# Four layers on one core: a feed-forward residual summed on GpSimd, displaced temporaries, and fewer GpSimd blocks in two selective scans

## The chip, the core and the metric

The kernel runs on one core of a Trainium2 chip. The metric is the device time of one execution in microseconds. A core has TensorE (PE in the profile, with its weight loads as PEld), VectorE (DVE), ScalarE (ACT), GpSimd (POOL) and SyncE (SP), which here only issues DMAs. All engines run their own instruction lists in order and wait for each other on semaphores. A TensorE result lands in PSUM; VectorE and ScalarE read PSUM, and GpSimd works on SBUF alone.

## The reference, cut to what matters

The input is an image batch of shape (4, 64, 128, 128) in float32, and four layers follow each other. Layer 0 is a state-space ("mamba") block with 16 states. Layer 1 is a windowed spectral mixing. Layer 2 is two 3x3 convolutions with a channel gate. Layer 3 is two convolutions, a mamba block with 64 states, and a feed-forward block. The change touches layer 0, the mamba block of layer 3 and the feed-forward block of layer 3.

```python
def step(h, inp):                       # over the 16384 positions of an image
    d_t, b_t, c_t, u_t = inp
    dA = jnp.exp(d_t[..., None] * A)                       # A: (128, states)
    h = h * dA + (d_t * u_t)[..., None] * b_t[:, None, :]
    y = jnp.einsum('bdn,bn->bd', h, c_t)
    return (h, y)
...
y = selective_scan(silu(conv(xin)), softplus(dt), A, Bm, Cm, D) * silu(z)
...
t = t + mamba(layernorm(t), ...)                           # layer 3
t = t + pvt2ffn(layernorm(t), ...)   # fc1, depthwise 3x3, gelu, fc2
return x + y                         # y: t as an image; x: the input of layer 3
```

The last line is the residual of the change: the feed-forward result has both `t` (kept in DRAM as `s3`) and the layer's input (`x3`) added to it.

## The kernel before

**The scans.** Class `_Mamba` serves layer 0 and layer 3. A chunk is 1024 positions; there are 64 chunks. The 128 inner channels are split into 4 quarters `j`, and the states are taken 4 at a time as a group `g`. One iteration is one pair (group, quarter), 128 partitions (4 states by 32 channels) by 1024 positions. A chunk of layer 0 has 4 groups and 16 iterations ("narrow"), a chunk of layer 3 has 16 groups and 64 iterations ("wide"). Each iteration needs these steps:

- ScalarE makes `da = exp(dl * A)` (L595), up to 7 buffers ahead.
- TensorE puts the input term `bx` into one of 3 PSUM tiles. In a group of kind "D" it spreads B over the partitions (L533) and VectorE multiplies by `du` (L539). In a group of kind "A" the products `bxT` were made beforehand in transposed form, and TensorE transposes them (L527).
- VectorE runs the recurrence as one scan over 1024 positions into one of 8 slots of `ring` (L640).
- GpSimd multiplies the scan's result by C, in the tile `cb` (L646), and after four iterations copies the last column to `state` (L648).
- TensorE sums over the states into `y` (L470), three iterations after the group ended.

**Who makes `bxT`.** A group's `bxT` has 8 blocks of 128 positions. For a whole block one GpSimd instruction serves all 4 states (L444); a block on ScalarE takes 4 instructions (L440). The list `mine` says how many of the 8 blocks GpSimd takes, by the distance of the group from the last "D" group. In layer 0 the kinds are D A D A and `mine` is (2,). In layer 3 they are D A A A four times and `mine` is (4, 2, 2), so 32 blocks a chunk. `run` paces the ScalarE part by a credit, so that it is done 4 iterations before its group.

**The pieces of the next chunk.** The convolution, the gates, the step size, B and C of the next chunk (`front`, `middle`), and the projection and norms of the last one (`behind`), are cut into pieces. The dictionary `slots` gives the iteration, relative to the chunk's first, at whose end a piece's TensorE part is issued; its ScalarE read follows one iteration later ("next"). A piece borrows one of the PSUM tiles from the `bx` pool (`take`, `give`). Where `slots` has "conv2", the convolution is issued in two halves. From the read of the convolution until the read of "v", `hold` keeps back the exponentials of L595. The order that `run` writes is pinned on each engine.

**Temporaries.** `tmp` hands out [128, 1024] tiles with one tag; some users split such a tile into two halves of 512 columns. `cb` is a tile of 1025 columns used from column 1. Tiles start on multiples of 32 bytes, so `cb` stands 4 bytes off `ring` modulo 32, while other operand pairs (`pos` and `xc` of L347, the halves of `nx` in L1527 and of `no` in L1566) stand a multiple of 32 bytes apart.

**The feed-forward block** (`layer3_ffn`). It works on 32 strips of 16 image rows. `first` computes fc1 of the strip after into `h1` and `h0`: GpSimd clears the edge columns (L1657, L1658), ScalarE writes the inside (L1671). `taps` does half of the depthwise convolution as 9 VectorE instructions (L1688, L1686); the other half runs on TensorE (L1735). `second` does fc2 and adds bias and residual on VectorE (L1701), then stores (L1704). The residual tile `res` is loaded by four DMAs from `s3` on SP; four DMAs issued by GpSimd add `x3` to it (both L1726), each after its load has landed. In SP's order a strip's stores (L1704) are followed by the load of `N` (L1645) and the loads of the next `res`. In GpSimd's order the four accumulating DMAs come before the memsets of the next `h1` and `h0`.

Of the kernel before, what the change touches and what calls it, by code (L numbers as in the profile page):

```python
# [10 lines left out]
F32 = mybir.dt.float32  # L11
AF = mybir.ActivationFunctionType
ALU = mybir.AluOpType
# [4 lines left out]
P = 128  # L18
B, C, HH, WW = 4, 64, 128, 128
HW = HH * WW  # L20
TC = 1024
# [149 lines left out]
class _Mamba:  # L171
# [131 lines left out]
        return self.wp.tile([P, w], F32, name=name, tag=name, bufs=bufs)  # L303

    def tmp(self, name):
        return self.wp.tile([P, TC], F32, name=name, tag="tmp", bufs=self.bufs["tmp"])


    def front(self, c, S, read, before_silu=None):
# [108 lines left out]
        self.read.add(id(t))  # L418

    def _C(self, c, g):  # L420
        t = self.t("cb", 3, TC + 1)[:, 1:]
        for q in range(NQ):
            n = NQ * g + q
            self.nc.sync.dma_start(t[DD * q : DD * (q + 1)], c["C"][n : n + 1, :].to_broadcast([DD, TC]))
        return t
# [266 lines left out]
@with_exitstack  # L692
def layer0(ctx, tc, K, w, x, x1):
    nc = tc.nc
    slots = {"conv": -24, "z": -22, "v": -20, "C": -16, "B": -14, "duT": -12, "project": 32, "rstd": 34}
    m = _Mamba(ctx, tc, K, 16, w, "DADA", {"xc": 2, "sz": 3, "tmp": 4, "bc": 2, "soon": (), "da": 7, "made": 0, "mine": (2,)}, slots)
    cp, wp = m.cp, m.wp
    eps = cp.tile([P, 1], F32, name="eps")
    nc.vector.memset(eps, 1e-5)
# [79 lines left out]
        finish.append(last)  # L779

    chunks = [{"at": divmod(i * TC, HW), "reset": i == 0} for i in range(B * HW // TC)]
    m.run(chunks, ahead, behind, 24)
    flush()


# [693 lines left out]
def layer3_mamba(ctx, tc, K, w, t3, s3, n3):  # L1479

    nc = tc.nc
    slots = {"centre": -47, "norm": -45, "conv": -32, "conv2": -31, "z": -30, "v": -29, "C": -16, "B": -14, "duT": -12, "project": 80, "centre2": 82, "norm2": 84}
    m = _Mamba(ctx, tc, K, 64, w, "DAAADAAADAAADAAA", {"xc": 1, "sz": 2, "tmp": 4, "bc": 1, "soon": (), "da": 7, "made": 7, "mine": (4, 2, 2)}, slots)
    cp = m.cp
    eps = cp.tile([P, 1], F32, name="eps3")
    nc.vector.memset(eps, 1e-5)
# [17 lines left out]
    def ahead(c):  # L1504
        if c is chunks[0]:
            load(c)
        t0 = c["at"][1]
        S = m.t("S", 1, TC + 3)
        no = m.tmp("nx")
        xs, sq = no[:, :512], no[:, 512:]  # L1510
        yield m.slot(c, "centre")
        pm = m.take(0)
        m.mm(pm, (K.cent, c["X"]))
        if c is not chunks[-1]:
            load(chunks[c["no"] + 1])
        yield "next", 0
        nc.scalar.activation(xs, pm, AF.Copy, scale=g1)
        nc.scalar.activation(sq, pm, AF.Square)
        m.give(pm)
        yield m.slot(c, "norm")  # L1520
        pm = m.take(0)
        m.mm(pm, (K.j2, sq))
        yield "next", 0
        _rstd(nc, sq, pm, eps)
        m.give(pm)
        yield "next", 0
        nc.gpsimd.tensor_mul(xs, xs, sq)  # L1527
        nc.gpsimd.tensor_copy(S[:, :3], tail if t0 else pad.to_broadcast([P, 3]))
        for h in range(2):
            nc.gpsimd.tensor_copy(tail[64 * h : 64 * (h + 1), : 3 - h], xs[64:, 509 + h :])  # L1530
        yield "next", 0
        yield "next", 0
        for k in range(2):
            for h in range(NH):
                at = 3 - k + 512 * h
                nc.sync.dma_start(S[64 * k : 64 * (k + 1), at : at + 512], xs[64 * h : 64 * (h + 1)])
        yield from m.front(c, S, lambda: None)

    def behind(c, yg):
        b, t0 = c["at"]  # L1540
        tr = m.tmp("tx")[:, :512]
        for h in range(NH):
            nc.sync.dma_start(tr[64 * h : 64 * (h + 1)], _halves(t3[b], t0)[h])
        yield m.slot(c, "project")
        pm = m.take(1)
        m.project(pm, woT, yg, tr)
        yield "next", 0
        nc.scalar.copy(tr, pm)
        m.give(pm)
        yield m.slot(c, "centre2")  # L1550
        pm = m.take(1)
        m.mm(pm, (K.cent, tr))
        yield "next", 0
        no = m.tmp("no")
        xs, o = no[:, :512], no[:, 512:]
        nc.scalar.copy(xs, pm)
        nc.scalar.activation(o, pm, AF.Square)
        m.give(pm)
        yield m.slot(c, "norm2")
        pm = m.take(1)  # L1560
        m.mm(pm, (K.j2, o))
        yield "next", 0
        _rstd(nc, o, pm, eps)
        m.give(pm)
        yield "next", 0
        nc.gpsimd.tensor_mul(o, xs, o)  # L1566
        for h in range(NH):
            nc.sync.dma_start(_halves(s3[b], t0)[h], tr[64 * h : 64 * (h + 1)])
            nc.sync.dma_start(_halves(n3[b], t0)[h], o[64 * h : 64 * (h + 1)])

    chunks = [{"at": (b, t0), "reset": t0 == 0} for b in range(B) for t0 in range(0, HW, TC)]
# [4 lines left out]
def layer3_ffn(ctx, tc, K, w, n3, s3, x3, out):  # L1576
# [4 lines left out]
    nc = tc.nc  # L1581
# [134 lines left out]
    for n, (b, r0) in enumerate(strips):  # L1716
# [4 lines left out]
        ahead = first(n + 1, H)  # L1721
        res = wp.tile([P, 2, 4, WW], F32, name="res3", tag="res3", bufs=3)
        ximg = x3[b].rearrange("c (r w) -> c r w", w=WW)
        for eng, img, add in ((nc.sync, simg, ALU.bypass), (nc.gpsimd, ximg, ALU.add)):
            for q in range(R // 4):
                eng.dma_start(res[half[q % 2], q // 2], img[:, r0 + 4 * q : r0 + 4 * q + 4, :], accum_op=add)  # L1726
        g0 = [wp.tile([P, 4, WW], F32, name=f"g0{q}", tag=f"g0{q}") for q in range(NR)]
        o = wp.tile([P, 2, 4, WW], F32, name="o3", tag="o3")
        pd = [dp.tile([P, 4, WW], F32, name=f"pd{q}", tag=f"pd{q}") for q in range(NR)]
# [127 lines left out]
```

## Time and profile before

| what | us |
|---|---|
| median of 3 runs (lowest, highest) | 17136.39 (17125.25, 17164.81) |
| the profiled execution, its own time | 17161.19 |
| its span, first to last instruction | 17159.4 |
| layer 0's scan, window 77 to 3185 | 3108 |
| layer 3's scan, window 5153 to 16065 | 10912 |
| feed-forward block, window 16160 to 17159 | 999 |

The profiled execution lies 24.80 us above the median, and 1.79 us of its time lie outside its span. Busy time is read stage by stage, since the stages have different limits. An instruction's duration can overlap the next one's by some tens of ns, so sums of durations come out a little above busy time. The page calls ScalarE's and VectorE's waits by the last releaser that it can see.

### The profile page before, as it was taken

The page shows a single profiled execution, that of the slowest core. Times are in us where ns is not written, and L with a number is a line of the kernel's source. Part 1 is how long each engine was busy: PE and PEld are TensorE (multiplying, and loading weights), DVE is VectorE, ACT ScalarE, POOL GpSimd, SP SyncE. Part 2 cuts the span into 40 slices and gives each one's busy share as a digit, 9 for nine tenths or more (in the row PEclk, how much of TensorE's full clock was granted, in tenths as well). Part 3 has the DMA queues.
Part 4 walks back from the last instruction along what each step waited for, and adds up shares of the span by engine and source line. Part 5 has one row for each costly group of instructions (what it writes and reads, how often), then busy time and mean ns, then how long its engine had stood idle before and what let it go on. Part 6 is the DMA issues. An engine that isn't in the chain of part 4 may idle for free.

```text
span 17159.4 us, 249842 instructions
## 1 busy us (share of the span) xinstructions
PE 13728.5 (80%) x85562; PEld 7134.6 (42%) x85562; DVE 15207.3 (89%) x8587; ACT 13644.9 (80%) x27884; POOL 13844.1 (81%) x9954
## 2 busy tenths in 40 slices
PE   7888888899987777777777777777777777777766
PEld 3333333388434444444444444444444444444312
DVE  7999999732879999999999999999999999999766
ACT  7888888411539999999999999999999999999532
POOL 6888888501449999999999999999999999999511
PEclk8888888889999999999889999999999999999888
DMA  6666666311343333333333333333333333333233
GB/s 161 175 174 175 173 176 176 105 43 44 119 141 91 97 85 96 87 96 86 96 86 96 88 96 86 98 89 93 89 94 90 93 90 94 91 92 89 66 67 66
DMA packets 705600, 1779.59 MB, mean 104 GB/s; under 512 B 202481, under 2 KB 246465, under 8 KB 694849
## 3 DMA queue, kind: packets, MB, share of 16 engines
q1 hardware_dynamic: 694080, 1746.83, 37.4%
q0 software_dynamic: 10240, 16.79, 0.7%
q8 instruction: 672, 11.01, 0.3%
q14 instruction: 608, 4.97, 0.1%
HBM read 1439.91 MB, written 289.41 MB: 101 GB/s over the span
## 4 chain that ended last, share of the span: by engine, by line
PE 32%; DVE 26%; ACT 15%; issue 10%; DMA 7%; POOL 4%; SPq 4%; DVEq 0%; POOLq 0%; ACTq 0%
DVE ring L640 18%; ACT bxT L440 7%; PE y L470 7%; PE bx L527 6%; PE bx L300 5%; ACT da L595 5%; DVE bx L539 4%; DVE g L1686 3%; PE bx L533 3%; PE m L1247 3%; POOL ring L646 2%; DMA du<-d 2%; SPq L566 2%; DMA d<-pos 1%; DMA dl<-d 1%
## 5 line engine op out<-in xcount | busy, mean ns | idle before, releaser
L640 DVE TENSOR_TENSOR_SCAN ring<-da,state,bx 128x1024 f32<-128x1024 f32 x4848 | 11037.2, 2329 | 206.2 <-PE bx L527 110.3
L646 POOL TENSOR_TENSOR ring<-ring,cb 128x1024 f32<-128x1024 f32 x5120 | 10219.1, 2016 | 550.6 <-DVE ring L640 311.8
L440 ACT ACTIVATE bxT<-duT,BT 128x128 f32<-128x128 f32 x19456 | 6038.3, 389 | 23.7 <-PE bx L527 22.9
L595 ACT ACTIVATE da<-dl,A 128x1024 f32<-128x1024 f32 x5120 | 5732.2, 1139 | 362.6 <-DVE ring L640 347.0
L527 PE MATMUL bx<-cst,bxT 128*128 128x128 f32 x28672 | 4316.8, 298 | 1138.1 <-DVE ring L640 1047.7
L527 PEld LDWEIGHTS bx<-cst,bxT 128*128 128x128 f32 x28672 | 3771.9, 210 | 2616.7 <-DVE ring L640 1605.2
L470 PE MATMUL y<-ring,cst 128*32 128x512 f32 x20480 | 2971.1, 661 | 103.0 <-POOL ring L646 103.0
L444 POOL TENSOR_TENSOR bxT<-duT,BT 128x512 f32<-128x512 f32 x2304 | 2391.5, 1049 | 9.9 <-ACT BT L384 9.9
L533 PE MATMUL bx<-bc,spread 64*128 64x512 f32 (+1 forms) x6144 | 1810.0, 686 | 627.0 <-DVE ring L640 624.3
L539 DVE TENSOR_TENSOR bx<-du,bx 128x1024 f32<-128x1024 f32 x1536 | 1852.4, 1213 | 458.5 <-PE bx L533 315.6
L470 PEld LDWEIGHTS y<-ring,cst 128*32 128x32 f32 x20480 | 630.1, 117 | 1841.9 <-issue 1251.3
L533 PEld LDWEIGHTS bx<-bc,spread 64*128 64x128 f32 (+1 forms) x6144 | 523.3, 198 | 1730.3 <-DVE ring L640 1204.8
L300 PE MATMUL bx<-S,cw 128*128 128x512 f32 x1024 | 668.0, 813 | 376.4 <-DVE ring L640 363.2
L1726 POOL DMA_DIRECT2D res<-d_x x128 | 106.4, 1256 | 923.1 <-DMA res<-d_s 922.1
L1247 PE MATMUL m<-V,cw 64*64 64x512 f32 x6144 | 715.7, 604 | 87.9 <-POOL V L1233 49.0
L1137 POOL TENSOR_TENSOR xs<-xs,cl 128x1024 f32<-128x1024 f32 x32 | 75.9, 2372 | 795.8 <-DVE cl L1136 795.8
L1671 ACT ACTIVATE h<-ph,ff_fc_b 128x384 f32<-128x384 f32 (+1 forms) x384 | 200.4, 574 | 598.4 <-PE ph L1666 575.5
L640 DVE TENSOR_TENSOR_SCAN ring<-da,bx 128x1024 f32<-128x1024 f32 x272 | 602.6, 2267 | 20.4 <-PE bx L527 11.2
L1686 DVE SCALAR_TENSOR_TENSOR g<-h,dww,g 128x2048 f32<-128x2048 f32 x256 | 602.0, 2352 | 11.3
L300 PEld LDWEIGHTS bx<-S,cw 128*128 128x128 f32 x1024 | 257.3, 264 | 783.0 <-DVE ring L640 466.7
L1735 PE MATMUL pd<-h,diag 32*32 32x512 f32 x9216 | 376.9, 671 | 191.8 <-POOL h L1658 162.7
L1247 PEld LDWEIGHTS m<-V,cw 64*64 64x64 f32 x6144 | 331.4, 136 | 470.2 <-issue 342.9
(341 smaller groups left out, 10271.5 us busy)
## 6 DMA issues: line engine op xcount, KB each, us to landing
cb<-c SPq DMA_DIRECT2D x5120, 128.0 KB, 2.9
dl<-d SPq DMA_DIRECT2D x2048, 128.0 KB, 3.0
du<-d SPq DMA_DIRECT2D x2048, 128.0 KB, 3.8
d<-pos SPq DMA_DIRECT2D x128, 512.0 KB, 4.2
d<-u SPq DMA_DIRECT2D x128, 512.0 KB, 3.9
S<-nx SPq DMA_DIRECT2D x256, 128.0 KB, 2.4
S<-in_x SPq DMA_DIRECT2D x120, 256.5 KB, 4.1
res<-in_x SPq DMA_DIRECT2D x128, 128.0 KB, 2.9
```

Of the source, the lines that this page charges most:

```text
L300: self.nc.tensor.matmul(out[: l.shape[1], k : k + 512], l, r[:, k : k + 512], start=i == 0, stop=i == len(pairs) - 1)
L440: nc.scalar.activation(t[:, k, q].rearrange("p e j -> p (e j)"), c["duT"][:, k, :], AF.Copy, scale=c["BT"][:, k, n : n + 1])
L444: nc.gpsimd.tensor_mul(t[:, k].rearrange("p q e j -> p q (e j)"), c["duT"][:, k].unsqueeze(1).to_broadcast(shape), c["BT"][:, k, NQ * g : ...
L470: nc.tensor.matmul(c["y"][DD * j : DD * (j + 1), _COLS[h]], K.sel, hc[:, _COLS[h]], start=False, stop=u["g"] == self.ng - 1,)
L527: nc.tensor.transpose(bx[:, P * m : P * (m + 1)], v["bxT"][:, m, :, :, j].rearrange("p q e -> p (q e)"), self.K.eye)
L533: nc.tensor.matmul(bx[:, _COLS[h]], self.spread[v["g"]][r], self.rows(v["c"]["B"], h, 0), start=True, stop=True)
L539: nc.vector.tensor_mul(tiles[k], v["c"]["du"][j], tiles[k])
L595: nc.scalar.activation(das[nexp], v["c"]["dl"][k], AF.Exp, scale=self.A[:, k, v["g"] : v["g"] + 1])
L640: nc.vector.tensor_tensor_scan(hs, das.pop(i), tiles[i], 0.0 if u["c"].get("reset") else st, ALU.mult, ALU.add)
L646: nc.gpsimd.tensor_mul(hc, hs, u["cb"])
L1247: self.nc.tensor.matmul(p[k][i][half[h]], U[half[i], k, x, :], V[half[i], k, NP * h : NP * (h + 1), x : x + WW], start=x == 0, stop=x == 2,)
L1686: nc.vector.scalar_tensor_tensor(g1, tap, wk, g1, ALU.mult, ALU.add)
```

## The change

Five edits are made together.

1. In the feed-forward block `x3` is loaded by four more plain DMAs on SP into a new tile `xin` (used from column 2), and one GpSimd addition over [128, 1024] puts it into `res`. GpSimd issues no DMA there any more.
2. `tmp` tiles of layer 3 become 1025 columns wide and are used from column 1 (`shift` 1; 0 in layer 0). The tiles that were split into two halves are now split at column 513 (`split`), so that the halves stand 4 bytes off each other.
3. `cb` is used from column 2 of 1026.
4. `mine` becomes (1,) in layer 0 and (4, 1, 2) in layer 3: one GpSimd block a group in the narrow chunk, 28 blocks in the wide one. In the whole program L444 goes from 2304 to 1920 instructions and L440 from 19456 to 20992.
5. The slots: layer 0 gets "conv" at -25 and a "conv2" at -24 (it was whole, at -24), "v" goes from -20 to -21 and the lead from 24 to 26. In layer 3 "conv" and "conv2" go one iteration earlier, to -33 and -32, "project" from 80 to 76 and "centre2" from 82 to 80.

```diff
     def tmp(self, name):
-        return self.wp.tile([P, TC], F32, name=name, tag="tmp", bufs=self.bufs["tmp"])
+        k = self.bufs["shift"]
+        return self.wp.tile([P, TC + k], F32, name=name, tag="tmp", bufs=self.bufs["tmp"])[:, k:]
+
+    def split(self, name):
+
+        t = self.wp.tile([P, TC + 1], F32, name=name, tag="tmp", bufs=self.bufs["tmp"])
+        return t[:, :512], t[:, 513:]
...
     def _C(self, c, g):
-        t = self.t("cb", 3, TC + 1)[:, 1:]
+        t = self.t("cb", 3, TC + 2)[:, 2:]
...
 def layer0(ctx, tc, K, w, x, x1):
-    slots = {"conv": -24, "z": -22, "v": -20, "C": -16, "B": -14, "duT": -12, "project": 32, "rstd": 34}
-    m = _Mamba(ctx, tc, K, 16, w, "DADA", {"xc": 2, "sz": 3, "tmp": 4, "bc": 2, "soon": (), "da": 7, "made": 0, "mine": (2,)}, slots)
+    slots = {"conv": -25, "conv2": -24, "z": -22, "v": -21, "C": -16, "B": -14, "duT": -12, "project": 32, "rstd": 34}
+    m = _Mamba(ctx, tc, K, 16, w, "DADA", {"xc": 2, "sz": 3, "tmp": 4, "bc": 2, "soon": (), "da": 7, "made": 0, "mine": (1,), "shift": 0}, slots)
...
-    m.run(chunks, ahead, behind, 24)
+    m.run(chunks, ahead, behind, 26)
...
 def layer3_mamba(ctx, tc, K, w, t3, s3, n3):
-    slots = {"centre": -47, "norm": -45, "conv": -32, "conv2": -31, "z": -30, "v": -29, "C": -16, "B": -14, "duT": -12, "project": 80, "centre2": 82, "norm2": 84}
-    m = _Mamba(ctx, tc, K, 64, w, "DAAADAAADAAADAAA", {"xc": 1, "sz": 2, "tmp": 4, "bc": 1, "soon": (), "da": 7, "made": 7, "mine": (4, 2, 2)}, slots)
+    slots = {"centre": -47, "norm": -45, "conv": -33, "conv2": -32, "z": -30, "v": -29, "C": -16, "B": -14, "duT": -12, "project": 76, "centre2": 80, "norm2": 84}
+    m = _Mamba(ctx, tc, K, 64, w, "DAAADAAADAAADAAA", {"xc": 1, "sz": 2, "tmp": 4, "bc": 1, "soon": (), "da": 7, "made": 7, "mine": (4, 1, 2), "shift": 1}, slots)
...
-        no = m.tmp("nx")
-        xs, sq = no[:, :512], no[:, 512:]
+        xs, sq = m.split("nx")
...
-        no = m.tmp("no")
-        xs, o = no[:, :512], no[:, 512:]
+        xs, o = m.split("no")
...
         ximg = x3[b].rearrange("c (r w) -> c r w", w=WW)
-        for eng, img, add in ((nc.sync, simg, ALU.bypass), (nc.gpsimd, ximg, ALU.add)):
+        xin = wp.tile([P, 2 * 4 * WW + 2], F32, name="xin", tag="xin")[:, 2:].rearrange("p (k r w) -> p k r w", k=2, w=WW)
+        for t, img in ((res, simg), (xin, ximg)):
             for q in range(R // 4):
-                eng.dma_start(res[half[q % 2], q // 2], img[:, r0 + 4 * q : r0 + 4 * q + 4, :], accum_op=add)
+                nc.sync.dma_start(t[half[q % 2], q // 2], img[:, r0 + 4 * q : r0 + 4 * q + 4, :])
+        nc.gpsimd.tensor_add(res, res, xin)
```

## The prediction

> **What bounds the kernel now.** I read the busy time by stage first, because the page's shares mix stages.
>
> ```profile
> core 0: us, PE busy (x) PEld busy (x) DVE busy (x) ACT busy (x) POOL busy (x), PEclk, DMA share, GB/s
> 77.00:3185.00 3108.00, 2658.20 (x13595) 1192.22 (x13596) 2971.17 (x1599) 2705.88 (x5024) 2606.30 (x1718) 0.89 0.66 173
> 5153.00:16065.00 10912.00, 8574.23 (x49330) 4574.71 (x49330) 10466.92 (x5182) 10035.20 (x21672) 10583.78 (x7539) 0.91 0.34 91
> 16160.00:17159.00 999.00, 676.61 (x9836) 199.68 (x9832) 636.45 (x330) 310.84 (x498) 123.19 (x257) 0.83 0.32 66
> ```
>
> Layer 3's scan (170.6 us a chunk, 64 chunks) has three engines near their limit: POOL 97%, DVE 96%, ACT 92%. Nothing can push it below DVE's 10467 us, so the prize is DVE's idle time, 10912 - 10467 = 445 us. The waits of that window say who ends it.
>
> ```profile
> DVE bx L539 <- PE bx L533: 239.8, 218, 3.6
> DVE ring L640 <- PE bx L527: 112.0, 176, 1.6
> DVE ring L640 <- PE y L470: 60.9, 76, 2.0
> ```
>
> DVE never waits for POOL in name, only for PE. A timeline shows who stands behind PE (iterations 31 and 32 of a chunk).
>
> ```profile
> 10531.46 1.99 POOL L646 TENSOR_TENSOR ring<-ring,cb 128x1024 f32<-128x1024 f32 x1
> 10533.50 3.37 PE L470 MATMUL y<-ring,cst 128*32 128x512 f32 x10 [1.92 <-POOL ring L646]
> 10536.80 2.17 PE L533 MATMUL bx<-bc,spread 64*128 64x512 f32 x8
> 10538.16 1.23 DVE L539 TENSOR_TENSOR bx<-du,bx 128x1024 f32<-128x1024 f32 x1 [3.14 <-PE bx L533]
> ```
>
> PE stands 1.92 us at the y-sums of a product that POOL finishes late; the spreads behind them come late, and DVE idles 3.14 us. I sorted the trace's rows by place in the chunk, over chunks 4 to 59. POOL starts L646 0.1 to 0.4 us behind the scan in the "D" groups and falls behind in the "A" groups, by up to 7.6 us at iteration 30. DVE's idle there averages 1.72 us a chunk, 110 us in all. With the 60.9 us on y, 171 us of the 445 hang on POOL's lag. The rest lies where pieces borrow PSUM tiles: 1.92 us a chunk at iterations 34 to 37 (conv2, z, v) and 1.43 at 18 to 20 (project, centre2, norm2).
>
> The feed-forward block is different. Its DVE is only 64% busy. One strip:
>
> ```profile
> 16706.39 1.40 DVE L1701 SCALAR_TENSOR_TENSOR o<-po,fc2b__121306,res 128x512 f32<-128x512 f32 x2
> 16707.17 2.41 SPq L1704 DMA_DIRECT2D out<-o  x4
> 16709.67 1.19 SPq L1645 DMA_DIRECT2D N<-d_n  x2
> 16711.04 2.38 SPq L1726 DMA_DIRECT2D res<-d_s  x4
> 16715.93 3.31 POOL L1726 DMA_DIRECT2D res<-d_x  x4 [29.80 <-DMA res<-d_s]
> 16718.00 1.38 POOL L1657 MEMSET h<- 128x18 f32 x1
> 16719.41 1.29 DVE L1688 TENSOR_SCALAR g<-h,dww 128x2048 f32<-128x2048 f32 x1 [11.61 <-POOL h L1657]
> ```
>
> This is a ring: DVE's output, ten DMA issues on SP, the landing of `res`, POOL's accumulating DMAs, and only then the memset that the next taps need. DVE idles 11.6 us of each 33.4 us strip.
>
> **Feed-forward: plain loads and an addition.** SP issues four more DMAs before the landing that POOL waits for, at 2.38 us for four. By bytes it is the same: ten DMAs move 1.64 MB in the eight slices of 1 us that they fill, 205 GB/s, so 0.52 MB more take 2.5 us. I take 2.45. The last `res` load landed at 16716.94 (issued 16712.83, 4.11 us in the chain of waits), and DVE started 2.47 us later, over POOL's last DMA issue and the memset. In their place stands an addition (2.0 us, below), 0.05 us to start, and a memset. The L1657 memset takes 1.09 us here, behind DMA issues; the same 128x18 memset at L1318, behind none, takes 0.13. I take 0.14: 2.2 us together. So each strip loses 2.45 + 2.2 - 2.47 = 2.2 us, over the 30 strips that wait so: +66. At the end VectorE need not wait for the last accumulating DMA (5.19 us to land at 17148.20) but for 2.5 us of loads and a 2.0 us addition, about 3 us less: +63 together. Ends: 0 if the added loads land with the others; 3.5 us a strip, +105, if the addition takes the undisplaced 2.37 us and the memset stays at 1.09. Queued behind POOL's new wait are the memsets, and behind those DVE's taps and PE's L1735, as before.
>
> **Displacement.** Instructions with both inputs a multiple of 32 bytes apart: L347 takes 2371 ns for 1024 columns, L1527 and L1566 1285 and 1295 for 512, so about 209 ns and 2.11 ns a column. At 4 bytes apart L646 takes 2016 for 1024. At 8 bytes L1233 has a median of 2021 for 1040 columns, at 16 bytes L1235 takes at least 2391 for 1040, so an undisplaced rate again. Hence L347 in layer 3 saves 0.36 us, and L1527 and L1566 (1.77 ns a column, 1115 ns) 0.18 each. `cb` at 8 bytes: (2021 - 209) / 1040 = 1.74, times 1024 plus 209 is 1993, 0.02 less than now. I price it at -0.02; ends are L825's rate (3595 for 2048, 4 bytes the other way, -0.1) and L1235's (+0.34), far from it in distance.
>
> "GPSIMD Engine Reference" of the Trainium skill, section "Instruction dispatch", calls some 2.5 cycles an element a floor for two inputs (at the 1.2 GHz of its "Specifications", 2133 ns for 1024), since both share a read port. By that no displacement could help; of the relief of 1.65 us below only the block's 1.05 would be left, and the sum some 35 us worse, an estimate from that page. L646's 2016 ns lie under this floor, so the trace decides.
>
> **Blocks from POOL to ACT, layer 3.** POOL loses 4 blocks a chunk at 1.05 us, ACT gains 16 instructions at 5049.4 / 16384 = 0.308 us of busy time, 4.93 us a chunk, 315 us in all. In iterations 16 to 30 POOL's relief is one block, 0.36 of the two norms and twelve times 0.02: 1.65 us of the 7.6 us lag. That is more than the 1.46 us that PE stands there on average, so I take 1.4 us of the 1.72, 90 us, and half of the 60.9 us on y: -120. Ends: 0 and -171. What is late next is ACT.
>
> ```profile
> ACT da L595 <- DVE ring L640: 321.7, 254, 2.5
> ACT no L1556 <- PE bx L300: 108.0, 63, 3.2
> ```
>
> The first is ACT's true slack, being ahead by all its `da` buffers: 321.7 us against 315 of new work. So the blocks are paid at today's pace, and a shorter chunk must come out of ACT's waits for PE (bc, no, tx, sz, pos, duT: 488 us), which shrink when ACT arrives later. I charge +45; ends 0, and +175 if they don't shrink and the whole gain of this stage is lost.
>
> **Slots, layer 3.** conv2 two iterations ahead of z lets z find the tile that xc's read frees (PE waits for that 30 us today), and project, centre2 and norm2 spread over 4 iterations each. Of the 215 us at these places I take a quarter, -55. Ends: -215; +110 if the conv half, now at iteration 31, holds the first spreads of a "D" group as POOL does now. Layer 3: -120 + 45 - 55 = -130.
>
> **Layer 0.** Eight conv matmuls run 6.02 us in one piece, and DVE then waits for PE: 1.04 us a chunk, of 75.8 in the window. In halves I take two thirds, -45. ACT gains 8 instructions a chunk, 158 us in all, with only 25.2 us of slack; but it stands 193.4 us at xc and 123.6 at sz, which earlier halves shorten, and "v" one iteration earlier ends the hold on the exponentials sooner. I set these against each other at 0. POOL's two blocks hide behind its 16% idle. Ends for the stage: -95 (all waits on PE and ACT) and +130 (ACT's work unabsorbed).
>
> **Sum.** +63 - 130 - 45 = -112. On the profiled execution's 17161.19 that is 17049; its 24.8 us above the median taken off, 17024, rounded to 17025.
>
> **Rivals.**
> *ACT becomes the bound* (slower). Place: the `da` and `bxT` that L533, L527 and L539 need. From the point where ACT's work plus its waits fill the chunk, layer 3 gains 0 and layer 0's gain goes too; the feed-forward loss stays: 17136 + 63 = 17200, up to 17330 with layer 0's end. For it: slack 321.7 against 315. Against: ACT's `da` are never less than 5.0 us early in layer 3 by my sorting. Chance 0.25.
> *DVE's floor.* Relief and spacing work together and two thirds of the 445 us go, layer 0 gives 70: 17136 - 297 - 70 + 63 = 16832. For it: all waits end in PE. Against: an even load needs no waits at all. 0.11.
> *A draw.* Layer 3 gives half, layer 0 nothing: 17136 - 65 + 63 = 17134. 0.09.
> *Displacing `cb` does harm*, at L1235's rate: 0.34 us more on 64 products, POOL past DVE by some 13 us a chunk, +800. 0.02: 8 bytes has its own row.
> My forecast keeps 0.53.
>
> **The numbers.** A measurement of this kernel can tell about 0.2%, 34 us, from no change. The forecast and DVE's floor are faster, 0.64; the draw 0.09; the rest 0.27. The range runs from 16870, into the floor case, to 17220, through most of the ACT case. The forecast alone spans 16910 to 17100.
>
> **What would show it.** Right: L347 near 2.0 us in layer 3, L646 at 1.98 to 2.02; layer 3's window near 10780 with "PE y <- POOL ring" (98.1 us) cut to a third and "ACT da <- DVE ring" near nothing; the idle before the first tap near 13.8 us. Wrong: DVE's waits in layer 3 pass to ACT, or a strip gets shorter than 33.4 us.

## The result and the profile after

The changed kernel takes 17202.24 us (median, 17198.51 to 17211.86) against 17153.55 us of the kernel before in the same comparison: a ratio of 1.0035, 95% interval 1.0026 to 1.0044. It is slower by about 50 us, and not faster by 112. The profiled execution took 17206.38 us, its span 17204.5. The busy time by stage, in the windows that answer to those of before:

```profile
core 0: us, PE busy (x) PEld busy (x) DVE busy (x) ACT busy (x) POOL busy (x), PEclk, DMA share, GB/s
77.00:3179.00 3102.00, 2660.47 (x13595) 1151.12 (x13595) 2974.83 (x1599) 2858.83 (x5538) 2491.39 (x1590) 0.89 0.67 173
5147.00:16057.00 10910.00, 8458.70 (x49331) 4569.48 (x49332) 10454.43 (x5183) 10307.19 (x22695) 10315.27 (x7284) 0.92 0.34 91
16152.00:17204.00 1052.00, 674.72 (x9800) 198.74 (x9796) 637.42 (x330) 310.81 (x498) 81.89 (x167) 0.82 0.26 63
```

Layer 0 gained 6 us of the 45 forecast, layer 3's scan 2 us of the 130, and the feed-forward block lost 53 of the 63. From the start of the last scan to the end of the span it is 1094 us before and 1148 after. Work moved in layer 3 as planned: POOL went from 10584 to 10315 us, ACT from 10035 to 10307. The window did not follow. Its waits of DVE, with the total, the number and the longest:

```profile
DVE bx L545 <- PE bx L539: 163.8, 153, 2.0
DVE ring L646 <- PE y L476: 142.9, 75, 3.1
DVE ring L646 <- PE bx L533: 104.6, 91, 2.0
```

Of the wait for the spreads (L533 before, L539 now) 76 us went, and the wait for the y-sums (L476) grew by 82. By place in the chunk: DVE's idle at iteration 31 went from 1.72 to 0.96 us, at 44 from 0.77 to 2.35, and a chunk's sum from 6.96 to 7.26. The feed-forward strip shows every planned step:

```profile
16732.59 2.51 SPq L1731 DMA_DIRECT2D res<-d_s  x4
16735.19 2.46 SPq L1731 DMA_DIRECT2D xin<-d_x  x4
16740.65 2.00 POOL L1732 TENSOR_TENSOR res<-res,xin 128x1024 f32<-128x1024 f32 x1 [32.85 <-DMA xin<-d_x]
16742.59 0.13 POOL L1661 MEMSET h<- 128x18 f32 x1
16742.76 1.28 DVE L1692 TENSOR_SCALAR g<-h,dww 128x2048 f32<-128x2048 f32 x1 [13.28 <-POOL h L1661]
```

Four more issues in 2.46 us, an addition of 2.00, a memset of 0.13, and DVE idle 13.28 us in place of 11.61.

**How stages are compared below.** The profiled execution of the kernel before lies 14 us above its median in the next comparison (17147.28). Layer 0 and the feed-forward block repeat within 4 us where their code is the same; layer 3 does not (10911.6 and 10880.4 us in two profiles of one code). So layer 3 "by medians" is a kernel's median time less everything in its profiled execution that is not layer 3's scan: 10898 us before, 10905 after. By medians the two kernels of that one code stand at 10898 and 10893, so differences of some 5 us say nothing.

### The profile page after: what moved, and what is told of

Read it like the earlier page. It is cut to its first block, busy times and chain, and to the rows that moved or that the text cites. A ratio compares the mean times of both kernels' runs of the same rounds, so it can differ in the third digit from the quotient of the medians.

```text
span 17204.5 us, 250815 instructions
## 1 busy us (share of the span) xinstructions
PE 13614.3 (79%) x85562; PEld 7091.6 (41%) x85562; DVE 15198.6 (88%) x8587; ACT 14069.9 (82%) x29420; POOL 13413.4 (78%) x9474
## 4 chain that ended last, share of the span: by engine, by line
ACT 30%; PE 23%; DVE 23%; issue 10%; DMA 7%; SPq 4%; POOL 1%; DVEq 0%; POOLq 0%; ACTq 0%
DVE ring L646 14%; ACT bxT L446 14%; ACT da L601 11%; PE bx L533 5%; PE y L476 4%; DVE bx L545 3%; DVE g L1690 3%; DMA du<-d 3%; PE bx L300 2%; PE m L1253 2%; PE bx L539 2%; SPq L572 2%; DMA cb<-c 1%; PE p L1167 1%; DMA dl<-d 1%
## 5 line engine op out<-in xcount | busy, mean ns | idle before, releaser
L646 DVE TENSOR_TENSOR_SCAN ring<-da,state,bx 128x1024 f32<-128x1024 f32 x4848 | 11038.6, 2330 | 379.1 <-PE bx L533 194.9
L446 ACT ACTIVATE bxT<-duT,BT 128x128 f32<-128x128 f32 x20992 | 6503.5, 390 | 23.1 <-PE bx L533 22.4
L601 ACT ACTIVATE da<-dl,A 128x1024 f32<-128x1024 f32 x5120 | 5709.9, 1139 | 187.9 <-DVE ring L646 172.0
L533 PE MATMUL bx<-cst,bxT 128*128 128x128 f32 x28672 | 4342.4, 299 | 1211.9 <-DVE ring L646 971.6
L533 PEld LDWEIGHTS bx<-cst,bxT 128*128 128x128 f32 x28672 | 3790.2, 211 | 2746.6 <-DVE ring L646 1397.3
L476 PE MATMUL y<-ring,cst 128*32 128x512 f32 x20480 | 2926.2, 673 | 88.7 <-POOL ring L652 88.7
L539 PE MATMUL bx<-bc,spread 64*128 64x512 f32 (+1 forms) x6144 | 1863.8, 697 | 806.3 <-DVE ring L646 806.1
L450 POOL TENSOR_TENSOR bxT<-duT,BT 128x512 f32<-128x512 f32 x1920 | 1987.8, 1049 | 9.9 <-ACT BT L390 9.9
L476 PEld LDWEIGHTS y<-ring,cst 128*32 128x32 f32 x20480 | 634.5, 118 | 1724.0 <-issue 1260.1
L539 PEld LDWEIGHTS bx<-bc,spread 64*128 64x128 f32 (+1 forms) x6144 | 516.9, 200 | 1976.9 <-DVE ring L646 1587.9
L1732 POOL TENSOR_TENSOR res<-res,xin 128x1024 f32<-128x1024 f32 x32 | 66.0, 2062 | 1027.8 <-DMA xin<-d_x 996.9
L1253 PE MATMUL m<-V,cw 64*64 64x512 f32 x6144 | 715.8, 604 | 87.5 <-POOL V L1239 48.3
L646 DVE TENSOR_TENSOR_SCAN ring<-da,bx 128x1024 f32<-128x1024 f32 x272 | 602.1, 2268 | 28.6 <-PE y L476 12.4
L300 PE MATMUL bx<-S,cw 128*128 128x512 f32 x1024 | 481.7, 613 | 13.6 <-DMA S<-nx 7.6
L374 PE MATMUL bx<-xc,wboth 128*64 128x512 f32 (+1 forms) x512 | 338.8, 1019 | 144.2 <-DVE ring L646 143.1
```

The costliest lines, as they stand in the source:

```text
L300: self.nc.tensor.matmul(out[: l.shape[1], k : k + 512], l, r[:, k : k + 512], start=i == 0, stop=i == len(pairs) - 1)
L446: nc.scalar.activation(t[:, k, q].rearrange("p e j -> p (e j)"), c["duT"][:, k, :], AF.Copy, scale=c["BT"][:, k, n : n + 1])
L450: nc.gpsimd.tensor_mul(t[:, k].rearrange("p q e j -> p q (e j)"), c["duT"][:, k].unsqueeze(1).to_broadcast(shape), c["BT"][:, k, NQ * g : ...
L476: nc.tensor.matmul(c["y"][DD * j : DD * (j + 1), _COLS[h]], K.sel, hc[:, _COLS[h]], start=False, stop=u["g"] == self.ng - 1,)
L533: nc.tensor.transpose(bx[:, P * m : P * (m + 1)], v["bxT"][:, m, :, :, j].rearrange("p q e -> p (q e)"), self.K.eye)
L539: nc.tensor.matmul(bx[:, _COLS[h]], self.spread[v["g"]][r], self.rows(v["c"]["B"], h, 0), start=True, stop=True)
```

## Experiments: each part alone

**The feed-forward edit alone** on the kernel before (the last hunk of the diff).

> The kernel before with the feed-forward edit alone (plain loads into xin, one GpSimd addition). Theory A (the whole loss comes from the feed-forward block, the scans gain nothing): the time rises by the 54 us by which the stretch from the last scan to the end grew, to a ratio of 1.003; idle before the first tap near 388 us, windows of both scans within 5 us of before (3108 and 10912). Rival B (the parts of the scan edit lost as well, and the loss is shared): the ratio stays under 1.002. The prediction's own term was +63, 1.0037.

Measured: 17192.43 us, ratio 1.0029 (1.0017 to 1.0041); 1147 us from the last scan to the end, layer 0 at 3107 us, layer 3 at 10893 by medians. The whole loss stands here, and the scan edits together bring nothing.

**The blocks alone**: `"mine": (2,)` to `(1,)`, `(4, 2, 2)` to `(4, 1, 2)`.

> The kernel before with only the blocks moved: mine (1,) in layer 0, (4, 1, 2) in layer 3. Theory A (the blocks that went stood in iterations where GpSimd catches up anyway, so its lag at iteration 30 stays at 7.3 to 7.6 us): layer 3's window within 20 us of 10912, DVE's idle at iteration 31 of a chunk still 1.4 us or more, waits 'ACT da <- DVE ring' down from 322 to 190 us or less. Rival C (ScalarE becomes the bound; the relief works and ScalarE takes it back): idle at iteration 31 under 1.2 us, but waits of DVE or PE on ScalarE's da and bxT up by 60 us or more together, layer 3 at 10930 to 11000. The prediction's term was -120 + 45 = -75 in layer 3: 10837.

Measured: ratio 1.0004 (0.9995 to 1.0012), but that is two effects. Layer 0 fell from 3107 to 3053 us, while layer 3 rose from 10898 to 10960. There iteration 31 fell only from 1.72 to 1.47 us of idle time, 36 rose from 0.79 to 1.50 and 44 from 0.77 to 1.17. The idle time at 31 is theory A's, the time of layer 3 is rival C's.

**The slots alone.**

> The kernel before with only the slots, the split convolution of layer 0 and its lead moved. Theory A: the waits at borrowed PSUM tiles move with the pieces and keep their sum; layer 3 within 20 us of 10912, idle at iterations 33 to 37 and 18 to 20 redistributed, layer 0 within 10 us of 3108 (idle at its iteration 10 gone, new at 13). Rival D (the slots lose in layer 3 what the rest gains): layer 3 +40 to +110, most of it at iterations 18 and 44. The prediction's terms were -55 in layer 3 and -45 in layer 0.

Measured: ratio 1.0007 (0.9998 to 1.0016); layer 3 at 10914, of which iteration 44 has 2.25 us of idle time a chunk; layer 0 at 3101, with the wait at iteration 10 gone (1.04 to 0.04) and a new one of 1.43 at 13. Theory A held: a chunk's sum of idle time in layer 3 went only from 6.96 to 6.98.

**The displacement alone.**

> The kernel before with only the operands displaced (shift 1 in layer 3, the split at column 513, cb from column 2 of 1026). Theory A: pos and xc do not get faster in layer 3 (2.38 us), the two norms fall to 1.10 us, the product stays at 2.01 us; GpSimd's lag at iteration 30 falls by 0.4 us or less and layer 3 by 0 to 25 us. Rival E (displacing tiles costs something elsewhere, on ScalarE's or VectorE's accesses): layer 3 slower by 10 us or more, or some instruction on tmp tiles longer than before by over 3%. By the prediction's own steps the displacement alone gives some 0.6 us of relief, a third of -120: -40.

Measured: ratio 0.9983 (0.9974 to 0.9992), layer 3 at 10869, a gain of 29 us. The norms' products fell to 1.10 us; they start in iterations 21 and 23. Idle at 31 went from 1.72 to 1.06. L353, the product of pos and xc, did not get faster:

```profile
L353 POOL TENSOR_TENSOR u<-pos,xc 128x1024 f32<-128x1024 f32 x63 | 150.0, 2381 | 0.0
```

So the parts in layer 3 are +62, +16 and -29, together +49, and the changed kernel has +8. In layer 0 they are -54 and -6, and the changed kernel has -6. Neither sum adds up, and that had to be explained.

## Experiments: layer 0 and the feed-forward block

Three kernels changed one thing in each of two or three stages at once, since each stage is read by itself.

> Three edits on the kernel before, one to a stage, read stage by stage. Layer 3: mine (3, 2, 2), so 28 blocks as after the change, but the block goes from the group that is made in the last four iterations before a D group. Theory F (place decides: relief counts only in the A iterations ahead of a wait): GpSimd's lag at iteration 30 falls by about 1 us, DVE's idle at iteration 31 under 0.9 us, layer 3 30 to 60 us under before (by medians 10898); the rival (ScalarE's 16 instructions cost the same wherever they stand) has layer 3 at 10930 or more, as mine (4, 1, 2) alone had 10960. Layer 0: the convolution in halves, but v left at -20, two blocks a group. Theory G (v one iteration earlier stands on PE ahead of the transposes for iteration 13 and made the new wait of 1.4 us there): no wait at 13, layer 0 at 3107 - 64 x 1.0 = 3043 or less; the rival (the halves themselves bring it, by holding a PSUM tile longer) stays at 3100. Feed-forward: the accumulating DMAs of before stand behind the memsets of the next strip. If the memset behind GpSimd's wait is what DVE waits for, the 11.6 us before the first tap nearly vanish, 250 to 350 us in all; if the residual or PE is late anyway, under 60 us.

> Three edits on the kernel before, one to a stage. Layer 3: mine (4, 2, 1): 28 blocks, the one taken from the third A group. Theory F: its block stands in iterations 24 to 29 or 40 to 46, so the lag at 30 falls by up to 1 us, but ScalarE has no idle time in iterations 40 to 47 and makes the four instructions more there: DVE's wait at iteration 44 or 36 grows by 0.5 us or more; layer 3 between 10880 and 10930 (before 10898 by medians). Rival (the place doesn't matter): 10960 as with mine (4, 1, 2). Layer 0: the convolution in halves, v at -20, and one block a group. Theory G: the gain of the blocks (3053) and that of the halves add, 2990 to 3020; rival: 3100 as in the changed kernel. Feed-forward: the plain loads and the addition of the changed kernel, the addition behind the memsets of the next strip. As GpSimd's wait for the loads then holds up nothing, the stretch from the last scan to the end is the same as with the accumulating DMAs behind the memsets, within 15 us, and 250 to 350 us under 1094; rival: the ten or fourteen DMA issues on SP still set the pace, 1050 or more.

> The changed kernel with two edits undone, one to a stage. Layer 3: mine back to (4, 2, 2), so that displacement and slots stand without the blocks. If the three parts add, layer 3 is at 10898 - 28 + 16 = 10886 by medians (changed kernel: 10905, where the parts alone would give 10948); if the slots and the blocks help each other, 10900 to 10930. Layer 0: the convolution whole again, with v at -21 and one block a group. Theory G: v alone brings the wait at iteration 13, 3090 or more against 3053 with v at -20; rival (halves): 3060 or less. The feed-forward block is that of the changed kernel, 1148 us from the last scan to the end.

**Layer 0.** The two edits tried are `"v": -21` back to `-20` with the convolution in halves, and `"v": -21` with the convolution whole. The first gave 3050 us in both kernels, with one block a group or two, so the gains of the halves and of the blocks do not add (2990 to 3020 was expected with both); the second gave 3262, with a wait of 2.22 us at iteration 13. So v is the cause. In the changed kernel, iterations 12 and 13 of a chunk (PE, ACT and DVE rows):

```profile
1618.79 1.13 PE L333 MATMUL bx<-S,wz 64*128 64x512 f32 x4
...
1619.97 1.02 ACT L336 ACTIVATE sz<-bx 128x1024 f32<-128x1024 f32 x1 [2.06 <-PE bx L333]
...
1621.05 1.99 PE L300 MATMUL bx<-xc,wdt 128*128 128x512 f32 x4 [1.12 <-ACT sz L336]
...
1622.87 2.09 PE L533 MATMUL bx<-cst,bxT 128*128 128x128 f32 x16
...
1624.02 2.35 DVE L646 TENSOR_TENSOR_SCAN ring<-da,state,bx 128x1024 f32<-128x1024 f32 x1 [1.55 <-PE bx L533]
```

v's four matmuls (L300) wait for the tile that sz frees, run 1.99 us, and only then come the transposes (L533) that DVE needs. With v one iteration later (the kernel with the blocks alone) the transposes go first:

```profile
1546.12 1.13 PE L327 MATMUL bx<-S,wz 64*128 64x512 f32 x4
...
1547.18 2.42 PE L527 MATMUL bx<-cst,bxT 128*128 128x128 f32 x16
...
1549.44 1.88 PE L300 MATMUL bx<-xc,wdt 128*128 128x512 f32 x4
```

**Feed-forward.** In both kernels what adds `x3` moves behind the memsets of the next strip, in one the accumulating DMAs of before, in the other the addition of the changed kernel; the loads on SP stay where they were:

```diff
         for _ in ahead:
             pass
+        nc.gpsimd.tensor_add(res, res, xin)
```

With the accumulating DMAs behind the memsets the stretch takes 754 us in place of 1094, and with the addition 803, where the same within 15 us was expected. A strip is now bound by DVE, busy 687 of 751 us in the first and 736 of 801 in the second. The first row is that of the accumulating DMAs, the second that of the addition:

```profile
L1686 DVE SCALAR_TENSOR_TENSOR g<-h,dww,g 128x2048 f32<-128x2048 f32 x256 | 602.1, 2352 | 11.2
```

```profile
L1686 DVE SCALAR_TENSOR_TENSOR g<-h,dww,g 128x2048 f32<-128x2048 f32 x256 | 652.0, 2547 | 11.2
```

The addition now runs beside the taps. The 61 taps that overlap one take 3171 ns on average, the other 195 take 2352, and the addition itself takes 3.2 us (median) in place of 2.0. Over the 256 taps that is 195 ns each, 50 us, the whole difference of the two stretches. In the changed kernel, where the addition falls into DVE's idle time, all but 3 taps overlap none and take 2352 ns as with the DMAs. So the accumulating DMAs are the better way once nothing waits behind them.

**Layer 3 in the same kernels.** `mine` (3, 2, 2) gave 10980 and (4, 2, 1) gave 11114, both far above theory F's times, the second also above its rival's 10960; half of theory F fell. The relief worked where it was placed: with (3, 2, 2) the idle time at iteration 31 fell to 0.36 us. But 36 rose to 3.40. The wait behind it on PE, 31.5 us in the kernel before:

```profile
PE bx L327 <- ACT xc L321: 178.0, 63, 3.2
```

z (L327) stands at iteration 35 for ScalarE's read of the convolution (L321), which ScalarE reaches late; behind z in PE's order stand the transposes for iteration 36. ScalarE's new blocks are less than half of that lateness: with the same block left out by both engines (next section) this wait is still

```profile
PE bx L327 <- ACT xc L321: 112.5, 61, 2.0
```

What makes the rest of it, no run took apart. Without the blocks but with displacement and slots (mine back to (4, 2, 2)) layer 3 is at 10900, where the parts give 10886; so they do not add there either.

## Experiments: what a GpSimd microsecond is worth in layer 3

**Operands exchanged**: `tensor_mul(du, pos, xc)` to `tensor_mul(du, xc, pos)`, with the displacement alone.

> The kernel before with the displacement alone, and the operands of the product of pos and xc exchanged: the first input is then xc, on a multiple of 32 bytes, the second pos, 4 bytes on. Theory H (the direction counts: the second input has to stand behind the first): 2.38 us becomes 2.0 us, GpSimd's lag behind it falls by 0.37 us, layer 3 0 to 25 us below the 10869 of the displacement alone. Rival I (the pair's distance is right but the written tile, also 4 bytes on, collides): it stays at 2.38 us. Nothing else changes.

Measured: the product got faster,

```profile
L353 POOL TENSOR_TENSOR u<-xc,pos 128x1024 f32<-128x1024 f32 x63 | 126.0, 2000 | 0.0
```

2000 ns against 2381 in the order of the changed kernel. Theory H holds for the instruction, and fails for the time: layer 3 rose from 10869 to 10904. GpSimd does 0.38 us less a chunk, and the chunk takes 0.55 us more. Most of its chunks take exactly 170.7 us.

**Relief without the charge**: a block is left out by both engines, so part of the computation is missing. TensorE transposes another block in its place.

```diff
-        todo = [(k, q) for k in range(NB - mine) for q in range(NQ)]
+        todo = [(k, q) for k in range(NB - mine - self.out(g)) for q in range(NQ)]
```

> The kernel before with two edits, one to a stage. Layer 3: the block that mine (3, 2, 2) takes from GpSimd is left out altogether, so part of the computation is missing: ScalarE does not make it either, and TensorE transposes block 0 in its place. This is the relief without the charge; mine (3, 2, 2) with the charge stood at 10979 (before 10898 by medians). Theory L (relief ahead of iteration 31 is worth its 1.7 us, and the loss was ScalarE's reading of xc, 2.8 us late at iteration 35): no such wait, idle at 31 and 36 both under 0.9 us, layer 3 at 10750 to 10830. Rival (ScalarE was not the cause, the tile order at 33 to 36 is): 36 still 2 us or more, layer 3 10900 or more. Layer 0: one block a group as in the changed kernel, conv and v as before, and one VectorE reduction of 256 columns more a chunk (some 0.3 us) at iteration 5. Lock theory (the chunk stands at 14 windows of 3.413 us = 47.787 us and gives or takes idle time): 47.79 still. Linear: 48.1.

> As before it, with the block that mine (4, 1, 2) takes left out altogether (made by neither engine; TensorE transposes block 0 in its place). Theory L: the relief alone, standing in iterations where GpSimd catches up anyway, is worth little: idle at 31 stays at 1.2 to 1.7 us, layer 3 within 30 us of 10898; the rest up to the 10960 of mine (4, 1, 2) was ScalarE's charge. The prediction's step (relief of 1.05 us pays 1 us a chunk): 10834 or less. Layer 0: one block a group, and one VectorE reduction of 1024 columns more a chunk (some 1.1 us). VectorE is then busy 46.4 + 1.1 = 47.5 us of 47.79: the lock theory says 47.79 still or a jump to another ratio of the windows (48.64 is 57 windows in 4 chunks, 51.20 is 15); linear: 48.9.

Measured: layer 3 at 10900 and 10884 (before 10898). For the block that the change removed (4, 1, 2), the relief alone is worth 14 us and the charge on ScalarE 76 (10960 - 10884); here theory L held. Idle at 31 stays at 1.60: its place gives no relief there. For (3, 2, 2) theory L fell. The idle time at 31 did fall to 0.45, the charge is gone, and still nothing is gained, because the wait at 18 rose from 1.10 to 1.93, and 36, at 3.40 with the charge, is at 1.85, still above the 0.79 of before. Most chunks of the latter take 170.7 us again.

## The lock to TensorE's clock gate

170.7 us in most chunks of five kernels with different work (the blocks alone, the slots alone, without the blocks, the operands exchanged, the block left out) looks like a clock. The granted clock, which the trace records as the share of TensorE's full clock that it was given, has it: every grant, full or half, lasts a multiple of 3.413 us, and 170.67 is 50 of these windows. Layer 0 shows it best. Its chunk takes 47.79 us in four kernels of different work (the blocks alone, both with v at -20, and the one with a reduction more), and 14 windows are 47.787 us. In the kernel before it is 48.64, in cycles of four chunks (48.3, 48.0, 47.9, 50.3): 57 windows. With the convolution whole and v at -21 it is 51.20: 15 windows. The test was the VectorE work added to layer 0 in the two kernels above, at iteration 5 of each chunk:

```diff
+            if more is not None and i % per == 5:      # 2 or 8 times 128 columns
+                nc.vector.tensor_reduce(more, self.K.eye.unsqueeze(1).to_broadcast([P, 2, P]), AX.XY, ALU.add)
```

A reduction of 394 ns a chunk left the chunk at 47.788 us, one of 1194 ns gave 49.45 us, with chunks of 49.0 and 50.0 in turn (29 windows are 98.99). Linear growth would have been 48.2 and 49.0. Idle time alone could have taken in the first; the second made the chunk 1.66 us longer for 1.19 us of work.

The "TensorE: Matmul & The Clock Gate" page of the Trainium skill, section "What's actually happening", gives such a gate a free-running window of 4096 cycles at 1.2 GHz, 3413 ns, with full and half rate only; the traces agree. The page closes the gate after at least one idle window. Here a window need not be idle, and the measurement decides: in layer 3 of the kernel before, a window at full clock was followed by a half one in 334 cases; in them TensorE was busy for at most 1.86 us of 3.41, and for 1.95 or more in 95% of those that were followed by another full one (65 of these 1989 had 1.86 us or less, so the border is not sharp). In layer 0 the busy time does not tell: with the blocks alone, 109 of the 112 full windows before a half one were busy for 3.3 us or more, with 2.56 to 2.77 us of it in spreads over 16 partitions (L533, 16*128), and of the 451 that were followed by a full one only two had over 2.5 us of these. What the gate counts there no run took apart.

How this makes DVE wait, in the changed kernel around iteration 44 of a chunk:

```profile
9523.95 0.49 PE L533 MATMUL bx<-cst,bxT 128*128 128x128 f32 x1 [0.53 <-ACT bxT L446]
...
9525.12 0.92 PE L533 MATMUL bx<-cst,bxT 128*128 128x128 f32 x3 [0.68 <-ACT bxT L446]
9525.96 3.64 PE L476 MATMUL y<-ring,cst 128*32 128x512 f32 x16
...
9529.72 4.58 DVE L646 TENSOR_TENSOR_SCAN ring<-da,state,bx 128x1024 f32<-128x1024 f32 x2 [2.69 <-PE y L476]
```

and its gate windows (PEclk is the third number from the end):

```profile
9520.58:9523.99 3.41, 1.78 (x13) 1.44 (x12) 3.41 (x2) 3.41 (x10) 3.41 (x4) 1.00 0.32 82
9523.99:9527.40 3.41, 2.73 (x12) 1.06 (x16) 3.04 (x2) 3.41 (x7) 3.41 (x4) 0.50 0.28 81
9527.40:9530.81 3.41, 3.41 (x18) 1.47 (x11) 1.09 (x1) 3.41 (x8) 3.41 (x3) 0.50 0.00 0
```

PE waits for ScalarE's bxT, so a window has only 1.78 us of work; the next two are granted half; and the y-sums that free the ring's slot take 3.64 us in place of the 1.93 that the same 16 matmuls take where the gate stayed open (iteration 43 of another chunk):

```profile
10550.31 1.93 PE L476 MATMUL y<-ring,cst 128*32 128x512 f32 x16
```

Over 56 chunks, 92 half windows begin in iterations 42 and 43 of the changed kernel, and 42 in the kernel before.

**Keeping the gate open.** Zeros are added to y:

```diff
+            if zero is not None and i % per in range(39, 44):
+                for _ in range(2):
+                    nc.tensor.matmul(u["c"]["y"][:DD, :P], zero, self.K.eye, start=False, stop=False)
```

> The changed kernel with ten small TensorE instructions more a chunk in layer 3: at iterations 39 to 43, two matmuls that add zeros to 32 x 128 of y. Theory J (the clock gate): in the changed kernel the granted clock falls to half at iterations 42 and 43 in 43 and 49 of 56 chunks, where TensorE stands waiting for bxT, so that the y-sums take 3.1 us instead of 1.5 to 1.9, and the wait of 2.2 us at iteration 44 is that. The zeros keep TensorE busy: half clock at 42 and 43 in fewer than 10 of 56 chunks, the wait at 44 under 1 us, layer 3 at 10905 - 64 x 1.2 = 10830 or less, although TensorE does more. Rival K (only ScalarE's lateness with bxT counts): the wait at 44 stays at 1.8 us or more and layer 3 within 20 us of 10905. Second reading: chunks of exactly 170.67 us (50 windows of 3.413 us) become rarer if the lock to the gate's windows is broken.

Measured: 17114.33 us, 0.9988 of the kernel before (0.9979 to 0.9997); layer 3 at 10825 where the changed kernel has 10905, with more work on TensorE. No half window is left at 41 to 44; the wait for the y-sums is

```profile
DVE ring L653 <- PE y L476: 49.8, 70, 2.5
```

93 us less. Theory J held, and the chunks of 170.7 are gone.

The same with the zeros also at iterations 15 to 17 (four each), on the kernel before and on the one that leaves out a block:

> The kernel before with zeros added to y in layer 3: four small TensorE matmuls at each of iterations 15, 16 and 17, two at each of 39 to 43 (in the changed kernel those at 39 to 43 alone brought layer 3 from 10905 to 10822). Theory J (the clock gate sets part of the waits, before the change too): half clock at 16 to 18 and 41 to 43 nearly gone, the wait at 18 (1.10 us) and at 44 (0.67) shrink, layer 3 at 10800 to 10860 against 10898. Rival (the gate costs only where the change made TensorE wait): within 15 us of 10898, or above, by the 22 instructions' own time on TensorE.

> The kernel that leaves out the block of mine (3, 2, 2) (made by neither engine, part of the computation missing; TensorE transposes block 0 in its place) with the same zeros added to y. Without the zeros its layer 3 stood at 170.67 us a chunk, 50 windows of the clock gate, although DVE's idle at iteration 31 had fallen from 1.72 to 0.45 us: the waits at 18 and 36 grew instead, with half clock at iterations 17 and 18 in 56 of 56 chunks. Theory J: with the gate open there the relief comes through: wait at 18 under 1.2 us, layer 3 at 10780 to 10840. Rival (the order of tiles at 18 and 36 took the relief, not the clock): layer 3 within 20 us of 10900.

Measured: the kernel before falls to 17045.86, ratio 0.9943 (0.9930 to 0.9955), layer 3 to 10798. Leaving out the block brings it to 10745, below the range of theory J. So the same relief, worth nothing with the gate as it was, is worth 53 us with the gate held open: the clock took that part. The wait at 18, 1.93 us without the zeros, is down to 0.32 (0.51 in the kernel before with the zeros). The wait at 36 (1.69 us, against 0.91) stays and takes some 50 us of the relief, so the clock is not its cause; which of the borrowed tiles or ScalarE's reads is, no run took apart.

**Versions that beat both kernels.**

> A version put together from the parts that gained: the feed-forward block of before with its accumulating DMAs behind the memsets of the next strip (754 us from the last scan to the end), layer 3 with the displacement alone (10869), layer 0 with one block a group alone (3053). If the stages add: 17142 - 340 - 28 - 54 = 16720. If a stage loses its gain beside the others (other phase of the clock gate): up to 16800.

> The best version so far (16724: accumulating DMAs behind the memsets, displacement in layer 3, one block a group in layer 0) with the same zeros. Theory J: layer 3 at 10780 to 10830 against 10865, so 16640 to 16690. Rival: 16724 or more.

> The changed kernel mended at the places that the runs named: in layer 0 v back at -20 (3050 as with the halves and v at -20), in layer 3 the same zeros (10822 or less), in the feed-forward block the accumulating DMAs of before behind the memsets (754). If the stages add: 17202 - 52 - 85 - 394 = 16671; with the wait at iteration 18 shorter as well, down to 16600.

Measured: the parts that gained 16723.96 (ratio 0.9760, 0.9747 to 0.9774), with zeros 16613.17 (0.9692, 0.9678 to 0.9705), the mended change 16642.61 (0.9707, 0.9694 to 0.9720). The stages of the first add to within 5 us of the 16720 expected; the other two came out 27 us below the range and 28 below the 16671. Layer 3 by medians, with the zeros at the same iterations in all three, is 10798 in the kernel before, 10759 with the displacement alone and 10792 with the whole change. So with the same zeros the change is still worth only 6 us there, of the 130 forecast: blocks and slots take back 33 of the displacement's 39. In that version the clock still falls to half at iteration 43 in 25 of 56 chunks, and of the 1.44 us that DVE idles at 44, 0.68 are put down to ScalarE's bxT, so clock and charge both have a part in it; no run separates them.

## Why the prediction was wrong

- **Feed-forward, +63: right.** +54 measured. DVE's idle time before the first tap grew by 1.8 us a strip where 2.2 was summed. The addition and the memset are as priced; by the medians of 27 strips the longer issue costs 2.7 us in place of 2.45, and GpSimd starts 3.6 us after the last issue where 4.1 was taken, so the landing was priced too long. (The memset of before took 1.38 us in the row shown and 1.07 on average; the 1.09 named for it enters only the upper end.) What the prediction did not look for is that the same row gave away a gain six times as large: the memset needs nothing of the residual.
- **Displacement: right in size, wrong for L347.** The norms (1.10 us against 1.115) are as forecast, `cb` hardly moved (2014 ns, from 2016, against 1993), and the part alone brought -29 us. L347 was priced by distance alone and kept 2381 ns, since it was the first operand that was displaced. As it stands behind iteration 30, the sum did not count its 0.36 us.
- **The relief, -120: the failed step.** It summed 1.65 us of relief for GpSimd in iterations 16 to 30, and took 1.4 us of DVE's wait for it. GpSimd's lag at 30 fell by 0.3 us, from 7.6 to 7.3. In the kernel with the blocks alone, the four that left had stood at 1, 17, 33 or 34, and 49. The one at 17 is in the counted stretch, but at iteration 20 GpSimd has caught up before and after (it starts 0.1 us behind the scan), so nothing of it is left at 30. With that block left out by both engines the lag at 30 is still 7.6 us, and the gain 14 us; with the displacement's 29 that is 43 of the 120. And the working assumed that a microsecond less of DVE's wait at one place is a microsecond less of the chunk. The block of (3, 2, 2) left out at the right place took 1.3 us off the wait at 31, and the chunk stayed at 170.67 us until the clock gate was held open.
- **The charge, +45: too small, and priced by the wrong sum.** 321.7 us of waiting over a whole stage was set against 315 us of work. ScalarE's idle time of before stood mostly in the D groups (1.6 to 3.3 us each) and was 0 at iterations 40 to 47. Alone it cost 76 us.
- **Slots, -55: wrong.** +16 alone: the idle time at 34 to 37 fell by 1.3 us a chunk, as hoped, and that at 44 grew by 1.5.
- **Layer 0, -45: wrong by its cancelling term.** The halves did end the wait at 10 and the blocks cost nothing (3053 alone). "v one iteration earlier" was set at 0 against ScalarE's work; it put 2 us of matmuls ahead of the transposes of iteration 13. With v at -20 the stage gains 57.
- **The rival** "ACT becomes the bound" forecast 17200 and the same stages: layer 3 nothing, layer 0 nothing, the feed-forward loss left. Its mechanism is half of the truth. ScalarE holds more of the chain (30%, against 15% before), by making PE wait, and PE's idle time then costs clock. But ScalarE never filled the chunk (10307 us busy of 10910), and +16 of the slots and the v of layer 0 are no part of it, so that its number came within 3 us is partly luck.
- **Signs.** L646 (2014 ns) and the idle time before the first tap (13.3 us) came as said. L347 near 2.0 us did not; "PE y <- POOL ring" went from 98.1 to 84.5 us and not to a third, "ACT da <- DVE ring" from 321.7 to 172.0 and not to nothing. "DVE never waits for POOL in name" overlooked 5.4 us.

Open is why layer 0 gains 54 us by its blocks: the wait named "ACT da" at iteration 15 of its chunk (0.53 us) goes although ScalarE has more to do. That the chunk then stands at 14 windows is shown, how it gets there is not. Open is also how the three edits of layer 3 come to +8 where the parts give +49; by the runs above their waits depend on the gate's windows, but no run took that sum apart.

## What to carry to other kernels

Price a relief or a charge at the iterations where it lands, not over the stage: idle time that stands elsewhere pays for nothing. When an engine's queue holds a wait, look first at what is queued behind it that doesn't need it; here that was worth 340 us, six times the best trade between engines. Where TensorE's clock drops to half in every chunk, look whether the chunk's time is a whole number of gate windows: small gains can then vanish, parts need not add, and a few matmuls in idle time can be worth more than the work they cost.

## What the runs showed of the hardware

- In layer 3 of the kernel before, all 334 full windows of 3.413 us before a half one had at most 1.86 us of TensorE work; a window need not be idle to close the gate. In layer 0 windows busy for 3.3 us closed it too, most of that in matmuls over 16 partitions.
- A loop can lock to these windows: 0.39 us of added work changed nothing (47.788 us), and a chunk with 0.38 us of GpSimd's work removed took 0.55 us longer, at 170.67 us in 46 of 63 chunks.
- GpSimd's product of two [128, 1024] operands takes 2000 ns with the second input 4 bytes past a multiple of 32 and the first on one, and 2381 with the roles exchanged. That is no general rule of direction: L825 of the kernel before, whose first input stands 4 bytes past the second in rows of 65 columns, has the fast rate too (3595 ns for 2048).
- A GpSimd addition that takes 2.0 us alone takes 3.2 us beside VectorE's two-input taps and lengthens those it overlaps: 3171 against 2352 ns. By the sums here the 32 additions cost VectorE 50 us, some 1.56 us each. The "GPSIMD Engine Reference" page of the Trainium skill, section "Specifications", names such contention for VectorE instructions with two SBUF inputs, and gives no price.
